# A causal mask in a fused maximum on VectorE, and a linear attention whose quotient is a mean less a small term

## The chip, the cores and the metric

The kernel runs on one core of one Trainium2 chip. The metric is the device time of one execution in microseconds (us), the median of several runs; a lower time is better.

## What is computed

Two layers over x of shape (8, 512, 128), float32. Each adds an attention and a feed-forward block to x, each behind a layer norm without weights:

```
x = x + gelu(linear_attention(norm(x)))    # 16 heads of 64, elementwise state:
        Q = elu(q)+1, K = elu(k)+1
        KV = sum_s K*v ; Ksum = sum_s K
        attn = Q * KV / (Q*Ksum + 1e-6) ; out = attn @ wo + bo
x = x + fp4_feed_forward(norm(x))          # silu(gate)*up, blockwise FP4 in front of each product
x = x + causal_attention(norm(x))          # 16 heads of 8, softmax over the keys up to the query
x = x + mixture(norm(x))                   # 8 experts, top 2, low-rank parts per expert
```

Batch by batch there are 8 such chains; only the weights are shared.

## The kernel before

One planner, `Plan`, takes every operation as a step with an engine, an estimated cost and a rank (its place in the batch's time: each stage is given a lane and a stretch from `low` to `high`, in units of a batch). `Plan.ordered` then runs a list scheduling over the five engines: at each moment it takes the ready step with the lowest rank for which a buffer is free, and so fixes the order in which each engine gets its instructions and which buffer a step uses. Steps marked `either` go to VectorE or GpSimd, whichever the planner finds free. `Plan.kept_warm` puts filler matmuls (`mid<-zeros,ident`) into gaps that the plan shows on TensorE. Since every instruction is issued in `Plan.issue`, all of them have one line in the profile, L397, and are told apart by their tiles.

PSUM has eight banks: two `pair` tiles of two banks, one `mid` and three `ahead`; halves of a free pair are lent out as `ahead`.

The stages of batch b, which overlap with those of other batches:

- `linear_attention(b)`: `normed_T` (layer norm and transpose to `xnT`), then for each of 8 blocks of 128 features three matmuls (`wk`, `wv`, `wq`) into `ahead`, the feature map (two passes on ScalarE, one on VectorE), sums over the sequence in `accum_out`. `products` takes two blocks at a time: it forms both denominators `z0` and `z1`, their product `r`, one reciprocal of `r` on VectorE (in two halves), and then each block's numerator times the other's denominator times `r`. `linear_out` multiplies by `wk_o`, which is `wo` scaled by KV, and applies the GELU.
- `fp4_feed_forward(b)`: quantisation on VectorE and GpSimd, matmuls into `pair`.
- `causal_attention(b)`: four groups of four heads. `largest(n + 1, t, mx)` runs one group ahead: it computes the scores of the next group for one block of 128 queries (`pair<-qkT`, 32 rows), adds the causal mask to the diagonal block in PSUM with a bf16 matmul of the identity and `mask_q`, and takes the largest score of every query in a reduction on VectorE (`mx`). `to_queries` writes these maxima into the rows of `qkT` by DMA, so that `scores` (34 rows) gets score less maximum out of its matmul; `scores` then takes the exponential on ScalarE (`pr`) and clears the masked part on GpSimd. `mid<-pr,va` sums the values.
- `routed(b)` and `experts(b)`: the mixture, one batch later. In `experts`, `pu` is a matmul into `ahead`, read by two passes with `mk` and with their difference `dm`.

Loads are issued on SyncE's queue in the order of the code: x of batch 0, the weights of linear attention, `bo`, the FP4 weights, the attention weights, x of batch 1, the rest.

The mask in `largest` before:

```python
for h in range(2):
    nc.tensor.matmul(
        heads[:, h, :, ts(t, P)], ident16,
        mask_q.unsqueeze(1).to_broadcast([P, k, P]), start=False, stop=True,
        skip_group_check=True,
    )
nc.vector.tensor_reduce(
    mx[:, 2 * some[0] : 2 * some[-1] + 2, t].rearrange("p (i h) -> p h i", i=k),
    heads, AX.X, ALU.max, negate=True,
)
```

Of the kernel before, what the change touches and what calls it, by code (L numbers as in the profile page):

```python
# [17 lines left out]
P = 128  # L18
NB = 8
S = 512  # L20
# [14 lines left out]
NEG = -1.0e30  # L35

# [98 lines left out]
class Plan:  # L135
# [113 lines left out]
    def ordered(self):  # L249
# [14 lines left out]
        ready_at = {s: 0.0 for s in self.steps}  # L264
        waiting = {e: [] for e in self.engines}
# [13 lines left out]
        while done < len(self.steps):  # L279
            for e in self.HOP:  # L280
                while busy[e] <= now:
# [4 lines left out]
                    for s in sorted(  # L286
                        ready,
                        key=lambda s: (s.rank - (ahead if s.work > 0.6 * s.cost else 0.0), s.number),
                    ):
                        if s.port and port > now:  # L290
                            continue
                        asked = {}
                        for b in s.takes:
                            asked.setdefault(b.tag, []).append(b)
                        if not all(
                            all(b in turns[s.lane, t][-len(bs) :] for b in bs)
                            for t, bs in asked.items()
                        ):
                            continue
                        if all(  # L300
                            (t not in kept or stuck) and free.has(t, len(bs)) for t, bs in asked.items()
                        ):
                            best = s
                            break

                        kept.update(asked)
# [268 lines left out]

HURRY, LOW, MODEL = 0.3, 0.5, False
# [25 lines left out]
def cost(engine, method, out, ins, a, k):  # L602
# [19 lines left out]
    if engine == "vector":  # L622
        if method == "reciprocal":
            return 0.06 + n * 6.3e-3
        if method == "tensor_scalar":
            return 0.14 + n * 0.57e-3
        if method == "bn_stats":
            return 0.21
        return 0.12 + wide * 1.05e-3
# [16 lines left out]
LANES = ("linear", "fp4", "attention", "routing")  # L646
# [11 lines left out]
    ("qf", [P, S], 7, F32),  # L658
    ("z", [P, S], 3, F32),
    ("r", [P, S], 1, F32),  # L660
    ("y", [P, S], 2, F32),
    ("wk_o", [P, D], 5, F32),
# [17 lines left out]
    ("pr", [P, 2, S], 4, F32),  # L680
# [14 lines left out]
def block_kernel(  # L695
# [81 lines left out]
    with plan.span("loads", -3.0, -2.0):  # L777
# [4 lines left out]
        for i in range(4):  # L782
            cols = slice(256 * i, 256 * i + 256)
            for parts, name, w in zip(wqkv, "qkv", (wq, wk, wv)):
                parts.append(load(f"w{name}{i}", w[:, cols]))
            wo_sb.append(load(f"wo{i}", wo[cols].rearrange("(c p) o -> p c o", p=P)))
        bo_sb = load("bo_sb", bo.rearrange("(o i) -> o i", i=1))
# [18 lines left out]
        xs[1] = load_x(1)  # L806
# [21 lines left out]
    mask_q = const.tile([P, P], BF16, name="mask_q", tag="mask_q")  # L828
    dev.gpsimd.memset(mask_q, 0.0)
    dev.gpsimd.affine_select(  # L830
        out=mask_q, in_=mask_q, pattern=[[-1, P]], compare_op=ALU.is_ge,
        fill=NEG, base=0, channel_multiplier=1,
# [3 lines left out]

    rank = const.tile([P, NT, E], F32, name="rank", tag="rank")
    for e in range(E):
        dev.gpsimd.memset(rank[:, :, e : e + 1], float(E - e))
    eps_sb = const.tile([P, 1], F32, name="eps_sb", tag="eps_sb")  # L840
    dev.gpsimd.memset(eps_sb, 1e-6)
    one_sb = const.tile([P, 1], F32, name="one_sb", tag="one_sb")
    dev.gpsimd.memset(one_sb, 1.0)
# [84 lines left out]
    def linear_attention(b):  # L928

        xnT = normed_T(xs[b], "ahead", "xn", "xnT")  # L930
# [12 lines left out]
        def features(c):  # L943

            ks, kv, kb = (new("s1", [P, 1]) for _ in range(3))
            kf = elu(c, 1, wqkv[1], "kf", accum_out=ks)
            nc.vector.tensor_scalar(ks, ks, float(S), None, ALU.add)
            pw = new("ahead", [P, S])
            nc.tensor.matmul(
                pw, wqkv[2][c // 2][:, ts(c % 2, P)], xnT, start=True, stop=True  # L950
            )
            nc.vector.scalar_tensor_tensor(pw, kf, 1.0, pw, ALU.add, ALU.mult, accum_out=kv)

            nc.vector.tensor_scalar(
                kb, ks, bqkv_sb[:, 2, c : c + 1], kv, ALU.mult, ALU.add
            )
            qf = elu(c, 0, wqkv[0], "qf")
            nc.scalar.activation(qf, qf, AF.Identity, bias=one_sb)
            z = new("z", [P, S])
            nc.scalar.activation(z, qf, AF.Identity, bias=eps_sb, scale=ks)  # L960
            wk_o = new("wk_o", [P, D])
            nc.scalar.activation(wk_o, wo_sb[c // 2][:, c % 2, :], AF.Copy, scale=kb)
            return qf, z, wk_o

        def products(c):


            (q0, z0, w0), (q1, z1, w1) = features(c), features(c + 1)
            r = new("r", [P, S])
            nc.either.tensor_tensor(r, z0, z1, ALU.mult)  # L970
            nc.either.tensor_tensor(q0, q0, z1, ALU.mult)
            nc.either.tensor_tensor(q1, q1, z0, ALU.mult)
            for part in (slice(0, 256), slice(256, S)):
                nc.vector.reciprocal(r[:, part], r[:, part])
            nc.either.tensor_tensor(q0, q0, r, ALU.mult)
            nc.either.tensor_tensor(q1, q1, r, ALU.mult)
            return [(w0, q0), (w1, q1)]

        return [p for c in range(0, NC0, 2) for p in products(c)]

    def linear_out(b, pairs):
        y = new("y", [P, S])
        for half in range(2):
            po = new("ahead", [P, S])
            with together():
                for i, (wk_o, qz) in enumerate(pairs[4 * half : 4 * half + 4]):
                    nc.tensor.matmul(po, wk_o, qz, start=(i == 0), stop=(i == 3))
            if half == 0:
                nc.scalar.activation(y, po, AF.Identity, bias=bo_sb)
            else:  # L990
                nc.vector.tensor_tensor(y, po, y, ALU.add)
# [163 lines left out]
    def largest(n, t, mx):  # L1155

        w = (t + 1) * P
        for some in shared(w):
# [3 lines left out]
            with one_go():  # L1162
                for at, i in enumerate(some):
                    for h in range(2):
                        nc.tensor.matmul(
                            heads[:, h, at, :], duo(n, i)[stack(h), 0, ts(t, P)],
                            duo(n, i)[stack(h), 1, 0:w], start=(at == 0), stop=False,
                            skip_group_check=True,
                        )
                for h in range(2):  # L1170
                    nc.tensor.matmul(
                        heads[:, h, :, ts(t, P)], ident16,
                        mask_q.unsqueeze(1).to_broadcast([P, k, P]), start=False, stop=True,
                        skip_group_check=True,
                    )
            nc.vector.tensor_reduce(
                mx[:, 2 * some[0] : 2 * some[-1] + 2, t].rearrange("p (i h) -> p h i", i=k),
                heads, AX.X, ALU.max, negate=True,
            )
# [193 lines left out]
    def experts(b):  # L1373
# [5 lines left out]
        for i, a in enumerate((a1_sb, a3_sb)):  # L1379
            pu = new("ahead", [P, S])  # L1380
            nc.tensor.matmul(pu, a, tT, start=True, stop=True)
            for k, m in enumerate((mk[:, 0, :], dm)):
# [47 lines left out]

    def stage(lane, low, high, what, *args):
        with plan.span(lane, low, high):
            return what(*args)

    for b in range(NB):
        if b > 1:
            xs[b] = stage("loads", b - 2.0, b - 1.9, load_x, b)
        pairs = stage("linear", b - 1.5, b - 0.95, linear_attention, b)
        stage("out", b - 1.2, b - 0.85, linear_out, b, pairs)
# [80 lines left out]
```

## Time and profile before

| | before |
|---|---|
| median of 3 runs | 1170.35 us (1169.69 to 1170.44) |
| the profiled execution | 1182.29 us |
| its span, first to last instruction | 1180.6 us |
| mean granted TensorE clock | 0.972 of full speed |
| instructions in the span | 15119 |

The page names engines PE (TensorE's matmuls), PEld (TensorE's weight loads, which run beside matmuls), DVE (VectorE), ACT (ScalarE), POOL (GpSimd) and SP (SyncE). A group is one line of code, engine, operation and tile, with the count behind "x"; behind the first bar stand the busy time of all of them in us and the mean of one in ns, behind the second the idle time of the engine just before them in us and who ended it. `out<-in` names tiles. The chain that ended last is followed back from the last instruction, at each step to what released it. A table by windows gives the stretch, its length, and then the busy time of each engine, the granted clock, the DMA engines' share and GB/s.

### The profile page before, as it was taken

What the parts mean: (1) busy time and instruction counts of PE and PEld (TensorE: products, weight loads), DVE (VectorE), ACT (ScalarE), POOL (GpSimd) and SP (SyncE); (2) the same over time, 40 slices, a digit from 0 to 9 for tenths busy, and PEclk for the clock granted to TensorE, in tenths of its full rate; (3) what the DMA queues carried; (4) which work ended last, traced back from release to release, by engine and by line L of the source; (5) the groups of instructions that cost most, each with busy time, mean ns of one, the idle gap of its engine ahead of it and who ended that gap; (6) DMA issues with size and microseconds to landing.
All of it is one profiled execution on the core that took longest, in us unless ns stands there. A gap on an engine that the chain in (4) does not pass through costs nothing.

```text
span 1180.6 us, 15119 instructions
## 1 busy us (share of the span) xinstructions
PE 1081.1 (92%) x5109; PEld 507.6 (43%) x5109; DVE 838.8 (71%) x1849; ACT 637.0 (54%) x1084; POOL 620.3 (53%) x654
## 2 busy tenths in 40 slices
PE   6778878999899899989999999999999999999988
PEld 2233333444434445444544344354444455454454
DVE  5987878979888776876687666777767676557443
ACT  5677676687785534554455744645644344344321
POOL 3866755766666456435527353276533471342424
PEclk9889999999999999999999997999999999999999
DMA  7000002000200020102010200020002000210000
GB/s 226 1 1 0 1 34 73 2 19 19 90 19 19 20 83 26 37 19 90 19 37 19 90 19 28 19 91 19 19 29 90 19 19 29 90 47 19 1 9 9
DMA packets 30573, 44.33 MB, mean 38 GB/s; under 512 B 4192, under 2 KB 18464, under 8 KB 30496
## 3 DMA queue, kind: packets, MB, share of 16 engines
q1 hardware_dynamic: 30496, 43.37, 11.3%
q8 instruction: 40, 0.66, 0.2%
q14 instruction: 37, 0.30, 0.1%
HBM read 23.95 MB, written 18.87 MB: 36 GB/s over the span
## 4 chain that ended last, share of the span: by engine, by line
PE 54%; DVE 21%; ACT 14%; POOL 4%; issue 4%; SPq 2%; DMA 1%; POOLq 0%; ACTq 0%; DVEq 0%
PE ahead L397 27%; PE pair L397 20%; PE mid L397 7%; DVE r L397 4%; DVE mx L397 4%; ACT qf L397 2%; ACT pr L397 2%; ACT z L397 2%; DVE sc L397 2%; SPq L397 2%; DVE h L397 1%; ACT ahead L397 1%; DVE kf L397 1%; ACT kf L397 1%; DVE act L397 1%
## 5 line engine op out<-in xcount | busy, mean ns | idle before, releaser
L397 ACT ACTIVATE pr<-pair 128x1024 f32<-128x1024 f32 (+1 forms) x192 | 166.6, 879 | 187.4 <-PE pair L397 163.4
L397 DVE TENSOR_REDUCE mx<-pair 128x4 f32<-128x512 f32 (+2 forms) x192 | 196.8, 1040 | 80.4 <-PE pair L397 69.6
L397 POOL TENSOR_SCALAR_AFFINE_SELECT pr<-pr 128x256 f32<-128x256 f32 (+1 forms) x192 | 92.8, 486 | 241.4 <-ACT pr L397 238.8
L397 PE MATMUL pair<-qkT 32*128 32x128 f32 (+7 forms) x1024 | 179.4, 395 | 12.7 <-DVE mx L397 6.1
L397 PEld LDWEIGHTS pair<-qkT 32*128 32x128 f32 (+1 forms) x1024 | 87.0, 186 | 195.0 <-ACT pr L397 57.7
L397 POOL TENSOR_TENSOR act<-act,tw 128x512 f32<-128x512 f32 x64 | 81.4, 1272 | 104.3 <-DVE act L397 102.5
L397 DVE SCALAR_TENSOR_TENSOR act<-act,ahead 128x512 f32<-128x512 f32 x112 | 76.4, 685 | 57.0 <-ACT act L397 41.9
L397 DVE RECIPROCAL r<-r 128x256 f32<-128x256 f32 x64 | 109.6, 1732 | 7.7 <-POOL r L397 7.5
L397 PE MATMUL ahead<-um,b_sb 128*128 128x512 f32 x224 | 111.5, 602 | 0.2 <-DVE act L397 0.2
L397 PE MATMUL mid<-pr,va 128*10 128x512 f32 (+3 forms) x1024 | 97.2, 449 | 1.9 <-POOL pr L397 1.8
L397 POOL TENSOR_TENSOR qf<-qf,r 128x512 f32<-128x512 f32 x64 | 80.3, 1271 | 24.0 <-DVE r L397 11.7
L397 POOL TENSOR_TENSOR qa<-qa,qa 128x704 f32<-128x704 f32 (+2 forms) x54 | 80.1, 1483 | 22.7 <-DVE qa L397 19.3
L397 POOL TENSOR_TENSOR qf<-qf,z 128x512 f32<-128x512 f32 x64 | 81.3, 1284 | 0.0
L397 PE MATMUL mid<-zeros,ident 128*128 128x512 f32 (+7 forms) x172 | 69.4, 487 | 3.8 <-POOL zeros L855 3.8
L397 ACT ACTIVATE act<-ahead 128x512 f32<-128x512 f32 x56 | 33.3, 596 | 68.0 <-PE ahead L397 68.0
L397 POOL TENSOR_TENSOR r<-z,z 128x512 f32<-128x512 f32 x31 | 39.4, 1272 | 49.0 <-ACT z L397 46.4
L397 PE MATMUL ahead<-act,a_sb 128*128 128x512 f32 x128 | 64.3, 610 | 0.6 <-DVE ahead L397 0.6
L397 PE MATMUL ahead<-qf,wk_o 128*128 128x512 f32 x104 | 60.0, 691 | 4.9 <-POOL qf L397 3.8
L397 PE MATMUL pair<-mask_q,ident 128*128 128x128 bf16 (+1 forms) x384 | 62.6, 245 | 0.0
L397 ACT ACTIVATE ahead<-ahead,bqkv_sb 128x512 f32<-128x512 f32 x93 | 60.8, 654 | 0.0
L397 PE MATMUL ahead<-tT,w_sb 128*128 128x512 f32 x112 | 58.4, 603 | 0.0
L397 PEld LDWEIGHTS ahead<-um,b_sb 128*128 128x128 f32 x224 | 39.6, 190 | 41.3 <-issue 37.3
(232 smaller groups left out, 2046.1 us busy)
## 6 DMA issues: line engine op xcount, KB each, us to landing
stacks<-qk SPq DMA_DIRECT2D x32, 512.0 KB
qkT<-stacks SPq DMA_DIRECT2D x128, 128.0 KB
x<-in SPq DMA_DIRECT2D x8, 256.0 KB
qkT<-mr SPq DMA_DIRECT2D x128, 4.0 KB
out<-x SPq DMA_DIRECT2D x8, 256.0 KB
w_sb<-in SPq DMA_DIRECT2D x3, 256.0 KB
wq<-in SPq DMA_DIRECT2D x4, 128.0 KB
wk<-in SPq DMA_DIRECT2D x4, 128.0 KB
```

Source lines behind the costliest of these rows:

```text
L397: getattr(e, method)(*a, **k)
```

## The change

Five things are done together.

1. The causal mask leaves TensorE. The scores' matmuls are written without it; in its place, VectorE runs for each head and query block one `tensor_tensor_reduce` over the scores in PSUM and a slice of a constant tile `causal` in SBUF: it adds the two, multiplies by -1, writes the result back to PSUM and keeps the smallest value in `mx`.
2. Linear attention uses Q*KV/(Q*Ksum + e) = KV/Ksum - (KV/Ksum)*(e/Ksum)/(Q + e/Ksum). `mean` is KV/Ksum with the value bias; it no longer depends on the position, so its product with `wo` is one column per batch (`pc`, eight matmuls of one column). `part` is the small factor, and scales `wk_o`. The numerators' products with the other denominator go away; `z` is made in place in `qf`. The small per-feature numbers are kept in `heads`, two columns at a time, three products of them on GpSimd.
3. `normed_T` of linear attention is a stage of its own lane, `norm`, with rank b - 1.9 where it stood at the head of b - 1.5.
4. The planner prefers, by 0.15 of a batch, a step that is the last user of a PSUM buffer.
5. In `experts`, the matmul into `pu` waits for `dm`. The load of batch 1's x moves up behind the weights of linear attention. Buffers: `qf` 7 to 9, `wk_o` 5 to 8, `pr` 4 to 3, `z` gone, `heads` 15.

```diff
+        last = {
+            max(b.users, key=lambda u: u.number)
+            for s in self.steps for b in s.takes if b.tag in self.psum
+        }
...
-                        key=lambda s: (s.rank - (ahead if s.work > 0.6 * s.cost else 0.0), s.number),
+                        key=lambda s: (
+                            s.rank - (ahead if s.work > 0.6 * s.cost else 0.0)
+                            - (EMPTY if s in last else 0.0),
+                            s.number,
+                        ),
...
+        if method == "tensor_tensor_reduce":
+            return TTR + wide * 1.05e-3
...
-    mask_q = const.tile([P, P], BF16, name="mask_q", tag="mask_q")
-    dev.gpsimd.memset(mask_q, 0.0)
+    causal = const.tile([P, S], F32, name="causal", tag="causal")
+    dev.gpsimd.memset(causal, 0.0)
     dev.gpsimd.affine_select(
-        out=mask_q, in_=mask_q, pattern=[[-1, P]], compare_op=ALU.is_ge,
-        fill=NEG, base=0, channel_multiplier=1,
+        out=causal, in_=causal, pattern=[[-1, S]], compare_op=ALU.is_ge,
+        fill=NEG, base=S - P, channel_multiplier=1,
     )
...
-            kf = elu(c, 1, wqkv[1], "kf", accum_out=ks)
-            nc.vector.tensor_scalar(ks, ks, float(S), None, ALU.add)
+            kf = elu(c, 1, wqkv[1], "kf", accum_out=ks[:, c : c + 1])
...
-            nc.vector.tensor_scalar(
-                kb, ks, bqkv_sb[:, 2, c : c + 1], kv, ALU.mult, ALU.add
-            )
-            qf = elu(c, 0, wqkv[0], "qf")
-            nc.scalar.activation(qf, qf, AF.Identity, bias=one_sb)
-            z = new("z", [P, S])
-            nc.scalar.activation(z, qf, AF.Identity, bias=eps_sb, scale=ks)
...
+            nc.vector.tensor_scalar(ks[:, two], ks[:, two], float(S), 1e-15, ALU.add, ALU.max)
+            nc.vector.reciprocal(ks[:, two], ks[:, two])
+            nc.vector.tensor_scalar(ek[:, two], ks[:, two], 1e-6, None, ALU.mult)
+            for i in range(2):
+                nc.scalar.activation(z[i], z[i], AF.Identity, bias=one_sb)
+                nc.scalar.activation(z[i], z[i], AF.Identity, bias=ek[:, c + i : c + i + 1])
+
+            nc.gpsimd.tensor_tensor(mean[:, two], kv[:, two], ks[:, two], ALU.mult)
+            nc.gpsimd.tensor_tensor(
+                mean[:, two], mean[:, two], bqkv_sb[:, 2, two], ALU.add
+            )
+            nc.gpsimd.tensor_tensor(part[:, two], mean[:, two], ek[:, two], ALU.mult)
...
-            nc.either.tensor_tensor(r, z0, z1, ALU.mult)
-            nc.either.tensor_tensor(q0, q0, z1, ALU.mult)
-            nc.either.tensor_tensor(q1, q1, z0, ALU.mult)
...
-            nc.either.tensor_tensor(q0, q0, r, ALU.mult)
-            nc.either.tensor_tensor(q1, q1, r, ALU.mult)
+            nc.either.tensor_tensor(r, z[0], z[1], ALU.mult)
...
+                nc.either.tensor_tensor(z[i], z[i], r, ALU.mult)
...
+        pc = new("ahead", [P, 1])
+        with one_go():
+            for c in range(NC0):
+                nc.tensor.matmul(
+                    pc, wo_sb[c // 2][:, c % 2, :], mean[:, c : c + 1],
+                    start=(c == 0), stop=(c == NC0 - 1),
+                )
+        same = new("s1", [P, 1])
+        nc.vector.tensor_tensor(same, pc, bo_sb, ALU.add)
+        nc.scalar.activation(y, y, AF.Identity, bias=same)
...
-                            duo(n, i)[stack(h), 1, 0:w], start=(at == 0), stop=False,
+                            duo(n, i)[stack(h), 1, 0:w], start=(at == 0), stop=True,
...
+            for at, i in enumerate(some):
                 for h in range(2):
-                    nc.tensor.matmul(
-                        heads[:, h, :, ts(t, P)], ident16,
-                        mask_q.unsqueeze(1).to_broadcast([P, k, P]), start=False, stop=True,
-                        skip_group_check=True,
+                    nc.vector.tensor_tensor_reduce(
+                        heads[:, h, at, :], heads[:, h, at, :], causal[:, S - w : S],
+                        -1.0, -NEG, ALU.add, ALU.min, accum_out=mx[:, 2 * i + h, t : t + 1],
                     )
-            nc.vector.tensor_reduce(
...
             nc.tensor.matmul(pu, a, tT, start=True, stop=True)
+            plan.steps[-1].needs[dm.buf.writer] = True
...
-        pairs = stage("linear", b - 1.5, b - 0.95, linear_attention, b)
-        stage("out", b - 1.2, b - 0.85, linear_out, b, pairs)
+        normed[b] = stage("norm", b - NORM, b - NORM + 0.1, normed_T, xs[b], "ahead", "xn", "xnT")
+        mean, pairs = stage("linear", b - 1.5, b - 0.95, linear_attention, b)
+        stage("out", b - 1.2, b - 0.85, linear_out, b, mean, pairs)
```

## The prediction

> **What bounds the kernel now.** I read the page first (busy time by engine, then the chain that ended last), then a table of four windows, then the chain inside two of them, then the groups by shape.
>
> ```profile
> PE 1081.1 (92%) x5109; PEld 507.6 (43%) x5109; DVE 838.8 (71%) x1849; ACT 637.0 (54%) x1084; POOL 620.3 (53%) x654
> ...
> PE 54%; DVE 21%; ACT 14%; POOL 4%; issue 4%; SPq 2%; DMA 1%; POOLq 0%; ACTq 0%; DVEq 0%
> ```
>
> TensorE is busy 92% of the span, but that share is not all work. The fillers, matmuls of `zeros` that the planner puts into TensorE's gaps, are 69.4 us of it. Work is thus 1081.1 - 69.4 = 1011.7 us, and 1180.6 - 1011.7 = 168.9 us is filler or nothing. Where those lie is seen by windows; in the second fence, the columns before the clock are TensorE and GpSimd, of the fillers alone.
>
> ```profile
> core 0: us, PE busy (x) PEld busy (x) DVE busy (x) ACT busy (x) POOL busy (x), PEclk, DMA share, GB/s
> 0.00:180.00 180.00, 135.98 (x329) 57.12 (x330) 138.73 (x350) 127.30 (x229) 116.49 (x125) 0.92 0.16 49
> 180.00:420.00 240.00, 220.53 (x1051) 99.73 (x1049) 201.86 (x444) 165.26 (x287) 152.35 (x151) 0.99 0.09 28
> 420.00:1140.00 720.00, 688.14 (x3621) 332.47 (x3621) 482.93 (x1033) 338.55 (x559) 335.18 (x367) 0.98 0.12 40
> 1140.00:1180.60 40.60, 36.43 (x113) 18.26 (x111) 15.32 (x24) 5.85 (x10) 16.29 (x13) 0.96 0.02 7
> ```
>
> ```profile
> 0.00:180.00 180.00, 18.54 (x34) 7.01 (x34) 0.13 (x1) 0.92 0.16 49
> 180.00:420.00 240.00, 19.78 (x52) 8.08 (x52) 0.00 (x0) 0.99 0.09 28
> 420.00:1140.00 720.00, 27.17 (x80) 12.53 (x80) 0.00 (x0) 0.98 0.12 40
> ```
>
> Stage A (to 180 us) is linear attention of three batches without any scores: TensorE works 117.4 of 180 us, VectorE 77%. Stage B (to 420 us) has linear attention and causal attention together: TensorE works 200.8 of 240 us (84%), VectorE is busy 84%. Stage C (to 1140 us) is causal attention and experts: TensorE works 661 of 720 us (92%), VectorE 67%. So the busier VectorE is, the more TensorE loses: 16% at 84%, 8% at 67%. The chain says the same. Its first lines in stage A and in stage C:
>
> ```profile
> by line: PE ahead L397 12.4%; DVE r L397 11.2%; SPq L397 10.0%; ACT qf L397 7.3%; PE pair L397 6.0%; ACT z L397 5.0%; POOL qf L397 4.1%; issue 4.0%; ACT ahead L397 3.7%; DVE kf L397 3.0%; POOL r L397 2.8%; ACT kf L397 2.7%; ACT pair L397 2.
> ...
> by line: PE ahead L397 33.3%; PE pair L397 26.3%; PE mid L397 9.0%; DVE mx L397 3.3%; ACT pr L397 3.0%; issue 2.8%; DVE r L397 1.9%; DVE act L397 1.6%; DVE sc L397 1.3%; POOL qa L397 1.2%; POOL act L397 1.0%; ACT qf L397 0.8%; DVE h L397 0.
> ```
>
> In A no engine holds it; it hops between VectorE, ScalarE and GpSimd. In C it stays on TensorE, 69% in three lines.
>
> **The change, part by part.** The prices come from these groups:
>
> ```profile
> L397 PE MATMUL pair<-mask_q,ident 128*128 128x128 bf16 x256 | 37.0, 227 | 0.0
> L397 PE MATMUL pair<-mask_q,ident 128*128 128x256 bf16 x128 | 25.5, 282 | 0.0
> ...
> L397 PE MATMUL ahead<-gw_sb,tT 128*128 128x8 f32 x64 | 8.3, 255 | 1.3 <-ACT tT L397 1.3
> ...
> L397 DVE SCALAR_TENSOR_TENSOR ahead<-kf,ahead 128x512 f32<-128x512 f32 x44 | 30.2, 687 | 3.0 <-PE ahead L397 3.0
> ...
> L397 DVE TENSOR_TENSOR x<-ahead,x 128x256 f32<-128x256 f32 x30 | 12.5, 417 | 16.3 <-PE ahead L397 14.7 <-ACT mk L397 1.4
> ...
> L397 DVE DVE_READ_ACCUMULATOR ahead<-kf,ahead 128x1 f32 x44 | 6.2, 142 | 0.0
> ...
> L397 POOL TENSOR_TENSOR qf<-qf,z 128x512 f32<-128x512 f32 x64 | 81.3, 1284 | 0.0
> ```
>
> *Mask, TensorE.* 384 mask matmuls go, 37.0 + 25.5 = 62.5 us. They have 0.0 us idle before them, so they lie back to back with work: 14.8 us in stage B, 47.7 us in C by the same windows. Added: 64 one-column matmuls of `mean`. The nearest row is `gw_sb`, 64 matmuls of 8 columns with a new weight each, 8.3 us; less than nothing is excluded, since they are instructions that were not there. Net -54 us of TensorE work.
>
> *Mask, VectorE.* 192 reductions go (196.8 us). In their place stand 512 fused passes, one per head and query block (128 each of 128, 256, 384 and 512 columns), and 512 accumulator reads that the built stream shows behind them. No such pass is in the trace. The nearest rows are two-tensor passes with one operand in PSUM: 687 ns at 512 and 417 at 256 make 1.055 ns per column and 147 ns fixed, so 282, 417, 552 and 687 ns: 128 x 1938 ns = 248 us. An accumulator read is 142 ns where the pass writes PSUM, as here (73 us in all), and 82 ns where it writes SBUF (42 us). Added to VectorE: 248 + 73 - 197 = +124 us; low end 248 + 42 - 197 = +93; high end, by the slowest single two-tensor pass at 512 columns (`y<-y,y`, 759 ns, 0.14 ns per column more on 163,840 columns), +147. Less than nothing is excluded: the columns are the same and the instructions more. I take +124, by the row nearest in form. If the pass ran at half rate it would cost some 170 us more; no row suggests that.
>
> [...]
>
> *Linear attention.* Two of the three products in front of the reciprocal go: 64 on GpSimd, -81.3 us (57.5 us of all `qf` products lie in A, 59.0 in B). Added are 96 products of two columns on GpSimd; the rows at 512 columns (1272 ns) and 704 (1681) give 2.1 ns per column and 0.18 us fixed, so +18 us. GpSimd falls by 64 us, but it is 4% of the chain: only the links `POOL r` and `POOL qf` of stage A can give time back. VectorE: 64 scalings at 268 ns and 64 at 150 become 64 two-column ones at 150 and 32 reciprocals at 177, -11 us. ScalarE: the addition to `qf` loses its vector scale (814 against 718 ns, 64 times, -6 us) and two more passes per batch over `y` give most of that back. The product of VectorE's reciprocal is still waited for by the same matmul, `ahead<-qf,wk_o`.
>
> *Layer norm ahead, bank order, `dm` first, buffers, loads.* These move steps and remove none. The built streams show what comes of them: before the first `projected` matmul stand 60 feature matmuls instead of 72, half a batch of linear attention less, and the first scores come that much sooner. The next batch's norm (its statistics on VectorE, one power on GpSimd) now waits for nothing but `xn`. `x1` moved before `bo_sb` on SyncE's queue passes only bytes that fp4 weights need, later than linear attention. The `dm` wait holds one matmul whose reader waits for `dm` anyway; queued behind it on TensorE are other lanes' matmuls, which the planner orders around it: nothing, or up to 1 us per batch if `dm` (437 ns) is late. One `pr` buffer less (3 for 4): a buffer lives some 5 us and a group of four heads takes 27 us for six of them, so 30 of 81 us are used; nothing. The fillers grow from 27,520 to 34,112 columns, most of it in A and B: the planner sees more gaps there, not fewer.
>
> **The sum, against the profiled execution** (1182.3 us, of which 1.7 lie around the span; the median of the runs, 1170.35, is 0.99 of it).
> - A: three batches took from 16 to 170 us, 51 us each; half a batch less is -26 us if all of it shows, 0 if the moved work is paid in full later. I take -15.
> - B: VectorE 201.9 + 24% of 124 - 4 = 228 us of 240, 95% busy. It can't shrink by TensorE's 14.8 us; they become filler. At 95% busy it lasts 240 us (0), at today's 84% 228/0.84 = 271 us (+31). I take 91%, 250 us: +10.
> - C: TensorE's work 661 - 47.7 + 6 + 8 (the moved linear matmuls) = 627 us; VectorE 483 + 94 + 13 = 590 us, 82%. With today's loss of 8% it lasts 683 us (-37), with stage B's loss of 16% 746 us (+26). I take a loss of 10 to 11%, 700 us: -20.
> - Tail: experts only, 0.
>
> Sum -25 us: 1157 in the profile, 1145 for the median. What is late next is `DVE mx`: scores wait in their PSUM pair until four passes are through.
>
> **Rivals.** (1) *TensorE's saving comes in full*: -54 and -15, 1113 in the profile, 1102 median. For it: 69% of C's chain is on TensorE. Against it: VectorE at 84% already cost 16% in B. (2) *VectorE takes over and the kernel is slower.* Place: the two PSUM pairs in B and early C, which each pass holds until its read. It decides once VectorE's share in C passes what stage B shows it can bear, 84%. Price: B at 228/0.84 = 271 us (+31), C at 746 (+26), A -15: +42, 1212 median; half of that, if only B is held, is 1185. (3) *Nothing shows*: the mask matmuls' place is taken by fillers and idle time throughout, as the growth of the fillers hints, and A's half batch is paid back in C: -54 of work and +54 of gaps, 1170.
>
> **Chances.** The forecast 0.5, rival 1 0.2, rival 2 0.2, rival 3 0.1. A measurement of this kernel tells about 0.2% (2.3 us) from no change. Faster by more: 0.5 + 0.2 + half of rival 3 = 0.75; the same 0.05; slower 0.20. The range has to take the bounds of A, B and C around the forecast and most of rival 1 and the lower part of rival 2: 1105 to 1182.
>
> **What would show it.** Right: no `mask_q` rows; TensorE's work without fillers near 957 us; `DVE mx` near 320 us with its reads; VectorE 950 us, above 90% in the stretch where `qf` and `mx` are both at work; first scores 10 to 25 us earlier; GpSimd near 556. Wrong: a fused pass far off 282 to 687 ns; VectorE above 84% in C with TensorE waiting for `mx` (rival 2); fillers and idle above 223 us (rival 3); below 160 (rival 1).

## The result: slower by 0.8%, and the profile after

| | before | after |
|---|---|---|
| median of 17 runs each | 1172.0 us | 1182.96 us |
| the profiled execution | 1182.29 us | 1181.39 us |
| its span | 1180.6 us | 1179.7 us |

The ratio is 1.0082, 95% interval [1.0055, 1.0109]: the changed kernel is slower by 0.8%, where the forecast was 1145 us. The runs of either kernel lie in groups some 11 us apart, and the profiled execution of before fell into its longer one; the two traces are therefore of equal length, and what they show in stages is short of those 11 us.

The page of the changed kernel, its busy times and the chain that ended last by engine:

```profile
PE 1066.6 (90%) x4889; PEld 505.4 (43%) x4889; DVE 914.9 (78%) x2656; ACT 630.6 (53%) x1092; POOL 561.3 (48%) x686
...
PE 55%; DVE 29%; ACT 9%; issue 4%; POOL 2%; DMA 0%; POOLq 0%; DVEq 0%; ACTq 0%; SPq 0%
```

TensorE's busy time fell by 14.5 us only, VectorE's rose by 76, and VectorE's share of the chain rose from 21% to 29%, while ScalarE's fell (14% to 9%). The same three windows as before, then those of the fillers alone (TensorE is the first column of busy time, the clock the third from the end):

```profile
core 0: us, PE busy (x) PEld busy (x) DVE busy (x) ACT busy (x) POOL busy (x), PEclk, DMA share, GB/s
0.00:180.00 180.00, 129.90 (x359) 59.08 (x360) 139.16 (x328) 118.04 (x218) 88.99 (x130) 0.94 0.18 55
180.00:420.00 240.00, 217.15 (x972) 100.56 (x970) 207.90 (x590) 149.82 (x266) 118.64 (x147) 0.96 0.07 23
420.00:1140.00 720.00, 684.01 (x3450) 328.05 (x3449) 552.07 (x1716) 357.98 (x601) 337.36 (x398) 0.99 0.12 40
```

```profile
0.00:180.00 180.00, 21.18 (x42) 8.40 (x42) 0.13 (x1) 0.94 0.18 55
180.00:420.00 240.00, 31.43 (x76) 12.32 (x76) 0.00 (x0) 0.96 0.07 23
420.00:1140.00 720.00, 30.22 (x84) 12.74 (x84) 0.00 (x0) 0.99 0.12 40
```

With the tail the fillers are 85.7 us (before 69.4). TensorE's work without them is 1066.6 - 85.7 = 980.9 us, and filler or nothing is 1179.7 - 980.9 = 198.8 us (before 168.9). In the third window the work went from 661.0 to 653.8 us, and VectorE is busy 552 of 720 us, 77%.

Fixed windows hide that work moved between them, so here are windows by content: first from the first `projected` matmul of the attention to the first `to_model` matmul (stage B), then from there to the last batch's `to_model` (stage C). Before, and after:

```profile
170.20:356.70 186.50, 170.09 (x741) 76.39 (x741) 157.55 (x332) 139.37 (x246) 123.30 (x116) 0.98 0.12 41
356.70:1116.00 759.30, 726.62 (x3855) 346.82 (x3854) 522.61 (x1113) 369.12 (x609) 361.03 (x399) 0.98 0.12 39
```

```profile
155.00:359.50 204.50, 177.21 (x731) 81.33 (x730) 175.84 (x463) 138.28 (x249) 103.96 (x129) 0.97 0.11 37
359.50:1117.80 758.30, 723.48 (x3649) 342.41 (x3649) 592.53 (x1845) 386.16 (x647) 353.44 (x421) 0.99 0.12 39
```

The first scores come at 155.0 us instead of 170.2 (-15.2). B then takes 204.5 us instead of 186.5 (+18.0), C 758.3 instead of 759.3 (-1.0), and the tail is 2.6 us shorter. What A saved B loses again, and C has gained nothing from 47.7 us of mask matmuls less. The half batch of linear attention itself did not go to B: of the records of feature matmuls (`xnT` with `wk`, `wv`, `wq`) A has 120 instead of 144, B 126 instead of 124 and C 138 instead of 116. B does almost the same work in 18 us more; VectorE's busy time in it grew by 18.3 us (157.6 to 175.8).

Where VectorE's time went, by groups of the changed kernel (busy of all, mean ns of one, and idle before them):

```profile
L406 DVE CUSTOM_DVE_ANT_0 pair<-pair,causal 128x512 f32<-128x512 f32 x128 | 88.2, 704 | 15.1 <-PE pair L406 12.0 <-issue 0.4
...
L406 DVE DVE_READ_ACCUMULATOR2_ANT mx<- 128x1 f32 x512 | 72.5, 142 | 0.0
L406 DVE CUSTOM_DVE_ANT_0 pair<-pair,causal 128x384 f32<-128x384 f32 x128 | 71.7, 568 | 21.1 <-PE pair L406 15.5 <-ACT ahead L406 1.2 <-ACT hqT L406 0.9
L406 DVE CUSTOM_DVE_ANT_0 pair<-pair,causal 128x256 f32<-128x256 f32 x128 | 55.3, 432 | 16.7 <-PE pair L406 11.0 <-ACT qf L406 2.2
L406 DVE CUSTOM_DVE_ANT_0 pair<-pair,causal 128x128 f32<-128x128 f32 x128 | 38.2, 299 | 11.7 <-PE pair L406 8.4
...
L406 DVE TENSOR_SCALAR heads<-heads 128x2 f32<-128x2 f32 x64 | 30.6, 478 | 1.2
```

The four passes take 704, 568, 432 and 299 ns and their reads 142. The chain in the stretch from 180 to 420 us has `DVE pair`, the passes, as its third link, where `DVE mx` stood before. Before, then after:

```profile
by line: PE pair L397 16.9%; PE ahead L397 10.7%; DVE mx L397 10.0%; PE mid L397 7.2%; DVE r L397 6.0%; issue 5.4%; ACT qf L397 3.8%; DVE h L397 3.5%; DVE sc L397 2.8%; DVE kf L397 2.7%; ACT z L397 2.5%; DVE qf L397 2.5%; ACT kf L397 2.1%; 
...
by line: PE ahead L406 23.1%; PE pair L406 14.6%; DVE pair L406 12.7%; PE mid L406 7.8%; DVE r L406 5.3%; issue 5.1%; ACT pr L406 3.2%; ACT qf L406 2.7%; DVE h L406 2.6%; DVE heads L406 2.5%; DVE sc L406 2.4%; DVE qf L406 2.3%; DVE kf L406 
```

And TensorE's longest sums of waiting in the changed kernel (us in total, times, the longest). Before, these three were 5.0, 3.7 and 6.9 us.

```profile
PE ahead L406 <- DVE qf L406: 15.2, 9, 3.4
PE ahead L406 <- POOL hq L406: 12.7, 2, 10.7
PE pair L406 <- DVE mx L406: 9.9, 17, 1.6
```

The wait for `hq` is in the main a single one of 10.7 us, at 54 us, where a transposition for the feed-forward block stands first in TensorE's order and linear attention's matmuls stand behind it. It is in stage A.

### The profile page after: what moved, and what is told of

Its sections match the earlier page's. It is cut to its first block, busy times and chain, and to the rows that moved or that the text cites. A ratio compares the mean times of both kernels' runs of the same rounds, so it can differ in the third digit from the quotient of the medians.

```text
span 1179.7 us, 15552 instructions
## 1 busy us (share of the span) xinstructions
PE 1066.6 (90%) x4889; PEld 505.4 (43%) x4889; DVE 914.9 (78%) x2656; ACT 630.6 (53%) x1092; POOL 561.3 (48%) x686
## 4 chain that ended last, share of the span: by engine, by line
PE 55%; DVE 29%; ACT 9%; issue 4%; POOL 2%; DMA 0%; POOLq 0%; DVEq 0%; ACTq 0%; SPq 0%
PE ahead L406 33%; PE pair L406 15%; PE mid L406 7%; DVE pair L406 7%; DVE r L406 4%; ACT qf L406 2%; DVE sc L406 2%; DVE heads L406 2%; DVE qf L406 2%; DVE h L406 2%; ACT pr L406 1%; DVE kf L406 1%; DVE ahead L406 1%; DVE mx L406 1%; DVE qa L406 1%
## 5 line engine op out<-in xcount | busy, mean ns | idle before, releaser
L406 DVE CUSTOM_DVE_ANT_0 pair<-pair,causal 128x384 f32<-128x384 f32 (+3 forms) x512 | 253.2, 501 | 64.5 <-PE pair L406 46.8
L406 PE MATMUL pair<-qkT 32*128 32x128 f32 (+7 forms) x1024 | 172.4, 389 | 15.8 <-DVE mx L406 8.3
L406 PE MATMUL ahead<-um,b_sb 128*128 128x512 f32 x240 | 123.0, 610 | 1.8 <-DVE act L406 1.8
L406 DVE SCALAR_TENSOR_TENSOR act<-act,ahead 128x512 f32<-128x512 f32 x120 | 81.7, 684 | 44.3 <-ACT act L406 33.9
L406 PE MATMUL mid<-zeros,ident 128*128 128x512 f32 (+7 forms) x208 | 85.7, 495 | 4.5 <-POOL zeros L866 4.5
L406 DVE DVE_READ_ACCUMULATOR2_ANT mx<- 128x1 f32 x512 | 72.5, 142 | 0.0
L406 ACT ACTIVATE ahead<-ahead,bqkv_sb 128x512 f32<-128x512 f32 x102 | 67.2, 658 | 0.0
L406 PE MATMUL ahead<-xnT,wq 128*128 128x512 f32 x106 | 59.8, 647 | 7.2 <-DVE kf L406 4.6
L406 PE MATMUL ahead<-tT,w_sb 128*128 128x512 f32 x120 | 63.1, 608 | 2.1 <-ACT va L406 1.6
L406 PE MATMUL ahead<-xnT,wk 128*128 128x512 f32 x98 | 54.6, 640 | 4.8 <-ACT xnT L406 2.1
```

The costliest lines, as they stand in the source:

```text
L406: getattr(e, method)(*a, **k)
```

## The experiments

The theory that the runs were to test: the fused pass is what loses, and it does so by VectorE time in front of the PSUM pairs, while the mask matmuls that it takes off TensorE were worth much less than their rows. The rivals: the rest of the change loses (quotient, norm, preference, loads); or the planner, told 0.2 us of fixed cost per pass where pass and read take more, laid out a poor order; or any change of the steps draws a new order and this one was unlucky.

### Parts of the change

Before without the mask in the maximum, planned anew:

```diff
-  heads[:, h, :, ts(t, P)], ident16, mask_q...   # both matmuls
```

> The kernel before without the mask matmuls, and nothing in their place: the maximum is taken over all keys of the blocks, masked or not (the mask is cleared later anyway, and a maximum that is too large only scales numerator and denominator alike). Theory V (TensorE's 62 us were worth having and the fused passes on VectorE ate them): 25 to 45 us faster than before, about 1135. Theory W (the mask matmuls lay in slack that the pair banks set): within 10 us of before.

Measured: 0.9688 [0.9648, 0.9729], 1140.2 us, as theory V had it. How much of it is the matmuls and how much the new order is asked below.

The changed kernel with the plain reduction in place of the passes:

```diff
-  nc.vector.tensor_tensor_reduce(heads..., causal..., accum_out=mx...)   # per head
+  nc.vector.tensor_reduce(mx..., heads, AX.X, ALU.max, negate=True)
```

> The changed kernel with the plain reduction in place of the fused passes and no mask in the maximum: VectorE is rid of 512 passes and 512 accumulator reads for 192 reductions (326 us of rows for 197). Theory V: 1125 to 1140, some 50 us below the changed kernel. Theory W: 1170 to 1180. Theory L (the linear attention's new order or the planner's preference is what loses): no lower than the same edit on the kernel before, 10 us or more above it.

Measured: 0.9828 [0.9794, 0.9862], 1155.9 us. The passes cost 2.5% in the changed kernel when the planner may lay it out anew. But this is also 16 us above the same edit on the kernel before, which is what theory L expected: without any mask, the rest of the change loses.

Before with the passes alone (mask matmuls and reductions out, `causal` and the cost in, three `pr` buffers), and the changed kernel with the mask as before:

```diff
 e3, against before:
+  nc.vector.tensor_tensor_reduce(heads[:, h, at, :], heads[:, h, at, :], causal[:, S - w : S], ...)
-  nc.tensor.matmul(heads[:, h, :, ts(t, P)], ident16, mask_q...)
-  nc.vector.tensor_reduce(mx..., heads, AX.X, ALU.max, negate=True)
-    ("pr", [P, 2, S], 4, F32),
+    ("pr", [P, 2, S], 3, F32),
 e4, against the changed kernel: the first three lines the other way round
```

> The kernel before with the fused passes alone (pr has 3 buffers, for space, as in the changed kernel). Theory V: TensorE -62 and VectorE +128 us of rows cancel, 1165 to 1190. Theory L: the mask part alone is a gain, 1140 to 1155.

> The changed kernel with the mask back on TensorE and the plain reduction: what is left is linear attention, norm, the planner's preference and the loads. Theory V: 1160 to 1170, at or a little below before. Theory L: 1175 or more.

Measured: 1.0139 [1.0097, 1.0181] and 0.9925 [0.9891, 0.9958]. On before's kernel the passes alone lose 16 us (e3 also has one `pr` buffer less). The rest of the change gains 9 us with the mask on TensorE and costs 16 without any mask (e2 against e1), so its own sign is open; what a new order alone can do, below, is as large. Planned anew in the changed kernel, the mask matmuls are worth 11 us (e4 against e2) and the passes cost 30 (against e2).

The quotient of linear attention alone, on the kernel without a mask (four `pr` buffers; norm, the loads and the `dm` wait as before); then with the preference for bank-freeing steps on top:

```diff
 e10, against e1:
-            nc.either.tensor_tensor(q0, q0, z1, ALU.mult)
-            nc.either.tensor_tensor(q1, q1, z0, ALU.mult)
+            nc.gpsimd.tensor_tensor(part[:, two], mean[:, two], ek[:, two], ALU.mult)   # and the rest of point 2
 g1, against e10:
+                            - (EMPTY if s in last else 0.0),
```

> The kernel before without mask and with the new quotient of linear attention (its buffers, pr still 4), the rest as before: GpSimd loses 64 us, VectorE's few-column steps gain some 10, TensorE gains 16 (64 one-column matmuls). If the quotient is what made the rest of the change cost 15 us on the mask-free kernel: 1150 or more. If norm, the planner's preference or the third pr buffer did: 1130 to 1142.

> The best kernel so far (no mask in the maximum, new quotient, 1139 us) with the planner's preference for the last user of a PSUM buffer. The whole rest of the change cost 15 us on the mask-free kernel, the quotient none of it. If the preference is the cause: 1150 or more. If norm, loads and the third pr buffer are: 1132 to 1145.

Measured: 0.969 [0.9644, 0.9737] and 0.9815 [0.9761, 0.9868]. Against 0.9688 without it the quotient is worth nothing in these two plans, though GpSimd falls to 559 us. The preference costs 1.3% there. In the changed kernel it is the other way:

```diff
-EMPTY = 0.15
+EMPTY = 0.0
```

> The changed kernel without the planner's preference for the last user of a PSUM buffer (0 for 0.15 of a batch), the rest as it is. On the mask-free kernel the preference cost 1.3%. If it is a cost of its own: 1165 to 1175. If it was one order among others: anywhere from 1180 to 1220, as the two other orders of the changed kernel that were run.

Measured: 1.0249 [1.0202, 1.0297], slower by another 1.7%. Opposite signs in two kernels speak against a price of the preference as such and for a new draw of the order; neither was separated from the other.

### The planner's part

The planner told the fixed cost of a pass and its read by their rows (0.164 + 0.142 us):

```diff
-TTR = 0.2
+TTR = 0.31
```

> The changed kernel with the planner told what the fused pass really took there (0.31 us fixed, pass and accumulator read, where it assumed 0.20). Theory P (the plan misjudged VectorE, and the order is what loses): 10 us or more below the changed kernel. Theory V (it is VectorE's time itself): within 6 us of the changed kernel.

Measured: 1.0363 [1.0318, 1.0408]. This plan is 2.8% worse, so the run gives no support to a wrong cost as the reason. It doesn't exclude it: one plan is one draw, and since pass and read overlap, the time from pass to pass (0.39 us at 128 columns, 0.79 at 512) has a fixed part of some 0.26 us, not 0.31. How much an order is worth by chance was asked by a change of 0.01 us in the cost of an unrelated step, in before, in the changed kernel and in the one without a mask:

```diff
         if method == "bn_stats":
-            return 0.21
+            return 0.22
```

> The kernel before with one cost of the planner changed by 0.01 us (a layer norm's statistics, 0.22 for 0.21): the same instructions in another order. What this moves is the luck of an order, and a part of the change is not told from it below that. I expect within 8 us of before on either side.

> The changed kernel with one planner cost moved by 0.01 us (0.22 for 0.21 of a statistics pass), as was done with the kernel before (+0.6%). Another order of the same instructions. If the change loses by its operations: 1175 to 1195 again. If its 0.8% is the luck of one order: it may come out at 1165 or below.

> The kernel before without mask matmuls and with the same hundredth of a microsecond moved in the planner's costs as in the two other reruns. It tells how much of the 3.1% is one good order: by the mask put back into it, 15 us belong to the matmuls and 22 to the order. Then another order should come out near 1155 to 1170; if the gain is the matmuls', near 1140.

Measured: 1.006 [1.0029, 1.0091] for before, 1.0326 [1.0277, 1.0375] for the changed kernel (2.4% more than 1.0082), 0.976 [0.9719, 0.9802] without a mask (0.7% more). In the changed kernel this is more than either expectation had. The 0.8% of the result is thus no larger than the luck of one order. Its sign has more behind it: the five plans with passes lie at 1.008, 1.014, 1.025, 1.033 and 1.036, the three planned with mask matmuls at 0.993, 1.000 and 1.006, the five with neither at 0.969, 0.969, 0.976, 0.982 and 0.983. The groups do not overlap, though the first two come within 0.2% of each other, and these are few draws: below, before's computation reaches 0.981 in an order that was planned for another kernel.

### The same order, other instructions

To take the planner out, the instructions of a step were exchanged after planning, so that every engine keeps the order that the kernel before (or another) has; the traces show it kept. First, before's order without the mask matmuls; then with the passes in place of the reductions too (f2, as f4 and f5 below, has one `oT` buffer for two, to make room; the order stays, and ScalarE waits for matmuls 31 us in all before it writes `oT`, 29 with two buffers):

```diff
 f1, after the mask matmuls are planned:
+  plan.steps[-1].calls = [c for c in plan.steps[-1].calls if c[1][1] is not ident16]
 f2, besides, after the reduction is planned:
+  plan.steps[-1].calls = [("tensor_tensor_reduce", (heads[:, h, at, :], ...), {...}) for at, i in enumerate(some) for h in range(2)]
```

> The order of the kernel before, instruction for instruction and fillers too, and only the mask matmuls left out of it after the planner was done (the maximum runs over masked keys as well). So no luck of an order is in it. Theory V: most of the 62 us of rows come back, 25 to 45 us faster. Theory W: under 12 us, and the gain of the replanned kernel without mask (36 us) was mostly a better order.

> The same order, the mask matmuls left out and each reduction exchanged, after the planner was done, for its two or four fused passes and their reads. Against the kernel before it is the change's first part with no other order; against the run without mask it is the price of the passes alone. Theory V or H: 20 to 45 us above the run without mask, near before. Theory P (only a wrong order made the part lose): 15 us or more faster than before.

Measured: 1.0029 [0.999, 1.0068] and 1.0878 [1.0834, 1.0922]. Without its 384 mask matmuls the kernel is not faster at all; with the passes it is 99 us slower than that, far above the 20 to 45 us that two of the theories had. The page's busy line and the granted clock by slices of f1, then of f2:

```profile
PE 1062.9 (90%) x4725; PEld 495.8 (42%) x4725; DVE 839.1 (71%) x1849; ACT 636.6 (54%) x1084; POOL 620.6 (53%) x654
...
PEclk9989999999999899989999999899989977999999
```

```profile
PE 1120.2 (88%) x4725; PEld 511.2 (40%) x4725; DVE 916.2 (72%) x2681; ACT 640.2 (50%) x1084; POOL 621.9 (49%) x656
...
PEclk9879997998898897999999997899969868979999
```

TensorE has the same 4725 records of matmuls in both. In f2 they take 1120.2 us for 1062.9, and the mean granted clock is 0.911 for 0.960. Busy time times clock is 1062.9 x 0.960 = 1020.4 and 1120.2 x 0.911 = 1020.5: the whole 57 us are clock. The span grew by 97.1 us (1176.4 to 1273.5); the other 40 are gaps. TensorE's wait for the maxima, of f1 and of f2:

```profile
PE pair L397 <- DVE mx L397: 10.8, 19, 1.3
```

```profile
PE pair L397 <- DVE mx L397: 38.8, 59, 2.1
```

28 of the 40 us are this one wait. What happens to the clock is seen in windows of 4 us in f2, and in TensorE's timeline at that place (start, length, idle before and who ended it):

```profile
1016.00:1020.00 4.00, 1.91 (x10) 0.76 (x10) 3.86 (x12) 1.02 (x1) 3.05 (x3) 0.95 0.00 0
1020.00:1024.00 4.00, 4.00 (x14) 1.50 (x18) 3.50 (x18) 1.02 (x1) 1.64 (x2) 0.50 0.00 0
1024.00:1028.00 4.00, 4.00 (x17) 1.31 (x17) 0.76 (x3) 1.69 (x3) 2.23 (x4) 0.50 0.00 0
1028.00:1032.00 4.00, 4.00 (x20) 1.84 (x21) 1.85 (x8) 1.91 (x3) 2.74 (x3) 0.50 0.00 0
1032.00:1036.00 4.00, 4.00 (x15) 2.45 (x14) 2.54 (x7) 0.00 (x0) 0.03 (x1) 0.50 0.00 0
1036.00:1040.00 4.00, 4.00 (x20) 1.53 (x24) 2.04 (x6) 0.60 (x1) 2.66 (x3) 0.50 0.45 131
1040.00:1044.00 4.00, 4.00 (x29) 2.38 (x26) 2.51 (x5) 0.73 (x2) 2.06 (x2) 0.99 0.01 3
```

```profile
1016.63 1.13 PE L397 MATMUL ahead<-act,a_sb 128*128 128x512 f32 x2
1019.85 1.52 PE L397 MATMUL pair<-qkT 34*128 34x512 f32 x6 [2.09 <-DVE mx L397]
1021.30 2.08 PE L397 MATMUL ahead<-act,a_sb 128*128 128x512 f32 x2
```

One wait of 2.09 us for `mx` leaves TensorE 1.91 us of work in four, and the clock then stands at 0.50 for 20 us in which TensorE is busy all the time: 10 us of work lost behind 2 us of waiting. Stretches at a clock below 0.85, in such windows, number 12 in before, 12 in f1 and 31 in f2, with 30, 44 and 106 us of full clock lost in them. Most (51 of the 55) follow a window in which TensorE had gaps (under 3.7 us busy), but not each (some begin behind two full or nearly full windows), so the gap as the cause is what the traces suggest, and was not tried by itself.

Two more in the same order with the plain reductions, and about 130 us of unrelated VectorE work put behind each query block's reduction (f4) or ahead of it (f5), and once planned as a step of its own (e9):

```diff
+  nc.vector.tensor_reduce(jo[:, 0:busy], junk.unsqueeze(1).to_broadcast([P, busy, 32]), AX.X, ALU.max)
```

> The same order without mask matmuls, and behind each reduction one reduction of a constant tile, as long as what the fused passes and their reads add (4.06 us per group, 130 us in all): VectorE's time without a longer hold of the pair. Theory V: as the fused passes in this order, within 8 us. Theory H: within 12 us of the run without mask.

> The same, but the added reduction stands in front of the one that frees the pair, so that the pair is held longer by it. Theory V: within 5 us of the run with it behind. Theory H: 10 us or more slower than that one, near the fused passes.

> The kernel before without mask (as in the first experiment) and with four reductions of a constant tile per group added on VectorE, some 4.06 us per group and 130 us in all: as much VectorE time as the fused passes added, but none of it between a pair bank's matmuls and its release. Theory V (VectorE's time as such): back to 1180 to 1195, as with the fused passes. Theory H (the pair banks are held longer by each pass and its read): stays within 12 us of the kernel without mask, 1140 to 1152.

Measured: f4 1.0563 [1.0504, 1.0622], f5 1.0749 [1.0705, 1.0793], e9 0.9937 [0.9907, 0.9967]. VectorE's busy time grew by 111 us in f4 and f5 against f1; the passes, counted from pass to pass, occupy it 106 us longer than the reductions did. Against f1 (1178 us) the work alone costs 62 us, standing between scores and maximum 21 more, and the passes themselves (f2) another 16. So most of the loss comes without a longer hold of the pair, which theory H did not have, and the hold adds to it, which theory V did not have. TensorE's clock in the traces of f4 and f5 was 0.923 and 0.925 with waits for `mx` of 21.5 and 46.4 us; f4's trace is of its longest execution (1253 us), and the other five have 0.931 to 0.950. Planned around, the same work costs 29 us against e1 (1140 us), though VectorE is then busy 81%; that is between what the two theories had. The passes planned (e3 against e1) cost 53 us. The difference of 24 us may be the hold of the pairs, but that is argued: it is no larger than two draws of an order can differ, and e3 has one `pr` buffer less.

In the order that the planner made for the passes, with plain reductions in it:

```diff
+  for s in plan.steps[first:]:
+      s.calls = []
+  plan.steps[-1].calls = [("tensor_reduce", (mx..., heads, AX.X, ALU.max), {"negate": True})]
```

> The changed kernel's own order, instruction for instruction, with one plain reduction (no mask in the maximum) where the fused passes and their reads stood: the price of the passes without any replanning, in the order that was made for them. Replanned, the same exchange brought 2.5% (28 us). If the passes' time on VectorE is what ate the gain: 25 us or more below the changed kernel, 1155 or less. If the order would have to change to use it: above 1170.

Measured: 0.9934 [0.9904, 0.9963], 1168.8 us. The passes thus cost 1.5%, 17 us, even in their own order: less than the 25 us that were expected if the passes had eaten the whole gain, and more than the 0 to 15 us that the mask matmuls are worth in the two other fixed orders (f1, and g5 below). The page's first line:

```profile
PE 1067.0 (91%) x4889; PEld 507.2 (43%) x4889; DVE 840.2 (72%) x1824; ACT 630.3 (54%) x1092; POOL 562.0 (48%) x686
```

The busy time of TensorE is that of the changed kernel (1067.0, 1066.6); the span is 12.4 us shorter (1167.3), all of it gaps.

Last, the mask matmuls put back into e1's order, which gives before's computation in another order:

```diff
+  plan.steps[-1].calls.append(("matmul", (heads[:, h, :, ts(t, P)], ident16, mask_q...), {"start": False, "stop": True}))
```

> The order that the planner made without mask (the first experiment, 1140 us), with the mask matmuls put back into it after planning: the result is the reference's mask again, and TensorE has its 62 us of rows more in an order that does not know of them. If those rows cost time wherever they stand: 1170 or more, 30 us above the run without them. If the order was what gained: below 1155.

Measured: 0.9813 [0.9771, 0.9856], 1154.9 us. Of the 3.1% (37 us) by which e1 is faster than before, 1.9% (22 us) are its order and 1.2% (15 us) the mask. The pages of e1 and of g5:

```profile
PE 1042.6 (92%) x4737; PEld 484.2 (43%) x4737; DVE 830.3 (73%) x1850; ACT 636.1 (56%) x1084; POOL 619.5 (55%) x653
```

```profile
PE 1059.0 (92%) x5121; PEld 499.6 (43%) x5121; DVE 831.5 (72%) x1850; ACT 636.7 (55%) x1084; POOL 619.5 (54%) x653
```

At granted clocks of 0.974 and 0.989, work at full clock is 1042.6 x 0.974 = 1015.5 and 1059.0 x 0.989 = 1047.4 us: the mask matmuls are 31.9 us of it, and 15.5 come back as a lower clock, which leaves 16.4 of busy time. Before against f1 gives 1050.8 - 1020.4 = 30.4, of which 12 come back as clock and 14 as gaps.

## Why the prediction was wrong, point by point

The step that failed is the price of the mask on TensorE, -62.5 us (-54 net), taken as TensorE time that goes: it was worth 30 to 32 us of TensorE's work at full clock, and 0 to 15 us of the kernel's time. The price of the passes on VectorE was right (248 us forecast, 253 measured), and they cost 17 us in the changed kernel's own order, which is more than the mask matmuls were worth in any fixed order tried.

**The mask on TensorE (-62.5).** The rows added up to 62.5 us with no idle time before them, and I took this for time that would go. The rows of TensorE's groups add up to 1234.8 us in before, against 1081.1 busy on the page: each row counts time in which a neighbour's matmul ran too. Two pairs of kernels of equal order put the mask matmuls at 30 to 32 us of full-clock work, and at 0 to 15 us of time, since half or more of that comes back as lower clock and gaps. "Back to back with work" was right, but with them out of before's order TensorE's gaps grew by 14 us.

**The one-column matmuls (+8.3).** They cost twice that:

```profile
L406 PE MATMUL ahead<-heads,wo 128*128 128x1 f32 x128 | 16.2, 256 | 0.0
```

These 64 matmuls left 128 records, and `gw_sb`'s 64 records are 32 matmuls, four per batch: two records each. TensorE's work without fillers fell by 31 us, not 54.

**The mask on VectorE (+124).** The pass was priced well: 248 us forecast, 253 measured, 73 for the reads as forecast. The busy time rose by 76 instead of 113 for the whole change, since a read starts before its pass's record ends (starts 0.22 us apart at 128 columns, the pass 0.30 long). From pass to pass it is 0.39, 0.53, 0.66 and 0.79 us, 128 x 2.37 = 303 us for what took 197 as reductions.

**Stage A (-15).** Measured -15.2, with a single wait of 10.7 us for `hq` in it, which no term of the forecast held. The forecast was a point taken between 0 and -26, so that it came out to the microsecond is luck. The saving was not kept.

**Stage B (+10).** Measured +18 by content, inside the bounds (0 to 31). The forecast had VectorE packed more closely, 91% busy. It stayed at 84% before and 86% after: the stage grew by 18.0 us and VectorE's time by 18.3. TensorE's filler and idle time rose from 17% to 26% of the stage at nearly the same share of VectorE, so that share did not set it.

**Stage C (-20): most of the miss is here.** Measured -1. TensorE's work was to fall from 661 to 627 us and fell to 653.8 (the window from 420 to 1140 us). By the rows, 24 records of feature matmuls more stand there (14 us, forecast 8) and 6.9 us of one-column matmuls (forecast 6). By difference, an estimate, the mask matmuls of C were thus worth 28 us of work instead of 47.7. The loss on top was not the error: filler and idle time were 9.2% of the stage, below the 10 to 11% forecast. Still, the "law" that ties TensorE's loss to VectorE's share (16% at 84%, 8% at 67%) was made from two stages with different work, and it does not hold. e9 has VectorE 81% busy over its whole span and runs 29 us behind e1; f2 has it 72% busy and runs 99 us behind f1. What counted in these runs is first whether the order allows for the VectorE work (29 us against 62 for about the same work), and then how long it stands between scores and the bank's release (21 us).

**The rivals.** Rival 1 did not come: TensorE's work fell by 31 us and the time not at all. Rival 2 has the right sign, and its milder form, only B held (1185), comes nearest to the 1183 measured; the range, up to 1182, left it out. Its condition did not come: VectorE was 77 to 78% busy in C, not above 84%, and C did not grow. Rival 3 names the rest: filler and idle time grew by 30 us against 31 us of work saved, and A's half batch went to C. B longer and C unchanged together gave the +0.8%. e3 shows the form that the loss takes once it is planned:

```profile
PE 1074.9 (91%) x4823; PEld 500.9 (42%) x4823; DVE 905.4 (76%) x2681; ACT 639.6 (54%) x1084; POOL 622.4 (52%) x654
```

Against e1, also without mask matmuls, its span is 53.5 us longer: 32.5 us more fillers (109.2 against 76.7) and 21 us more idle time, at a better clock (0.983). TensorE's work without fillers is the same in both (966 us), so what the passes cost stands as fillers and idle time.

**Linear attention, buffers, norm, loads.** GpSimd 561 us for 556 forecast, its two-column products 202 and 195 ns on average for 185. The two-column scalings on VectorE took 478 ns instead of 150, 20 us more than forecast, between 99 and 1527 ns each; why is open. That the quotient takes nothing off the time was in the forecast. The rest of the change as a whole is worth -9 us in one pair of plans (e4) and +16 in another (e2 against e1).

**The reference time.** The profile of before was taken in an execution of 1182.3 us at a mean clock of 0.972; executions of the same kernel near 1170 us have 0.980 to 0.988. Its stage C holds this stretch:

```profile
720.00:740.00 20.00, 19.23 (x79) 7.00 (x77) 13.11 (x27) 6.86 (x10) 8.41 (x10) 0.64 0.01 3
```

At a clock of 0.64 it loses 7 us. Working from that profile made C look longer than the median run has it. That the whole difference lies in such stretches is argued from one trace.

**What stays open.** Whether the preference has a price of its own: it, or its draw, is 1.3 of the 1.4% by which e2 lies behind e10, which leaves next to nothing for norm, the loads, the `dm` wait and the `pr` buffer together in these plans. What the mask matmuls are worth in the changed kernel's own order, which was not run. How far a lower clock is cause and how far effect of gaps in the kernels planned anew.

The fastest kernels here are e1 and e10, 3.1% below before; they leave the mask out of the maximum, which holds as long as no masked score is far above the unmasked ones of its row, since the masked part is cleared later. With the whole computation of before, g5 is fastest, 1.9% below it and 2.7% below the changed kernel.

## What to carry to other kernels

Do not subtract a group's row from an engine's busy time: rows of neighbours overlap (1234.8 us of rows in 1081.1 busy), and the short matmuls here, back to back with others, were worth half of their rows in work and 0 to 15 of 62.5 us in time; compare the sum of the rows with the page's busy time first. What work moved to another engine costs is not told by that engine's share of busy time: here it was the order, and then the place between a bank's filling and its release. And with a list scheduler, measure a part in a fixed order and in several plans before crediting it with a per cent: 0.01 us in an unrelated cost moved the time by 0.6 to 2.4%.

## What was unexpected of the hardware

In f2 a wait of 2.09 us was followed by 20 us at a granted clock of 0.50 with TensorE fully busy. The same 4725 records of matmuls in the same order took 1063 to 1120 us of busy time at mean clocks of 0.960 to 0.911, and busy time times clock stayed within 0.3% (1020.4, 1020.5, 1022.8 and 1023.0 us in f1, f2, f4 and f5). Taking matmuls away went with a lower clock in the traces (0.989 to 0.974 in one order, 0.972 to 0.960 in the other): of the busy time that was saved, 15.5 and 12 us were lost again by it.
